# Two of the three inner dense layers of a graph-attention output stage by seven block products, and the last bias added to rows in DRAM

## The chip, the cores and the metric

The kernel runs on one NeuronCore of a Trainium2 chip. A core has a matrix engine (TensorE, PE in the profile; its weight loads are listed apart as PEld), a vector engine (DVE), a scalar engine that applies functions (ACT), a general engine that here mostly issues transfers (POOL, GpSimd), and an engine that issues transfers (SP). Each has its own instruction queue and works through it in order; they wait for one another by semaphores. Transfers go through 16 DMA engines. Data lies in DRAM, in the on-chip memory SBUF (128 partitions) and in PSUM, eight banks of 512 float32 per partition into which TensorE writes.

The metric is the device time of one execution in microseconds (us). Three runs of the kernel before gave 2115.71, 2116.22 and 2118.41 us; the median is 2116.22.

## The reference

Two residual layers on a graph of N = 3327 nodes with 1024 features. The first is a quantised graph convolution. The second, which the change touches, is a graph attention with 8 heads of 64 features, followed by four dense layers:

```python
def _L1_gnn_ref(x, adj, W, a1, a2, W1, b1, W2, b2, W3, b3, W4, b4):
    Wh = jnp.einsum('nf,hfd->hnd', x, W)
    ...
    att = jax.nn.softmax(e, axis=-1)
    h = jnp.einsum('hnm,hmd->hnd', att, Wh)
    h = jax.nn.elu(h)
    enc = jnp.transpose(h, (1, 0, 2)).reshape(x.shape[0], -1)   # 3327 x 512
    out = jax.nn.relu(enc @ W1.T + b1)                          # 512 -> 256
    out = jax.nn.relu(out @ W2.T + b2)                          # 256 -> 256
    out = jax.nn.relu(out @ W3.T + b3)                          # 256 -> 512
    out = out @ W4.T + b4                                       # 512 -> 1024
    return out
...
x = x + _L0_gnn_ref(h, adj, ...)
h = jnp.maximum(_layernorm(x, axis=-1), 0.0)
x = x + _L1_gnn_ref(h, adj, ...)
```

The result is x after the first layer (called x1 in the kernel, the other branch of the last addition) plus the output of the fourth dense layer with its bias b4.

## The kernel before

The 3327 rows lie in T = 26 tiles of 128. Three stages follow one another.

*First stage* (about 0 to 920 us): normalisation, quantised weights, and for each row tile the product with the adjacency matrix (L840) and the eight heads' products (L708). It writes x1 to DRAM as `x1_d`, tile by tile, on POOL's queue, and the heads' features and scores as `feat_d` and `src_d`.

*Attention* (about 895 to 1853 us). `attends` lists 8 heads times 4 sub-ranges of row tiles (7, 6, 7 and 6 tiles), 32 passes. Each pass goes through the 13 pairs of column tiles in 7 `GROUPS`. For a step (pass, group) the function `select` makes masks: ACT writes `over` (L969, two buffers of a pair each), DVE turns it into two selection tiles `sel` (L978 and L979, six buffers, one for a pair). `sums` multiplies the selections with the head's features on PE (L998) into one PSUM bank per row tile. `select` runs two steps ahead of `sums` (`AHEAD = 2`). When a pass ends, `closing` reduces the banks on DVE (L1017, L1022), applies the softmax's denominator and the ELU on ACT, and POOL's queue stores the encoded rows to `enc_d` (L1046). SP's queue loads the scores of the pass after the next (`load_src`, L933) and, once a head, the features of the next head (L918). The function `pin` chains the instructions of each engine in the order in which they are written out here; instructions outside `pin` are placed by the framework's scheduler. During the last pass SP loads what the output stage needs: encoded rows, x1 rows, weights, biases and, into `bb4`, the bias b4 broadcast to all partitions; two layers of group 0 are already computed between the sums (L1164), and `weight_sums` (L1196) makes differences of blocks of W4 on DVE.

*Output stage* (from 1853 us). The row tiles form 7 groups: 0 to 5 of four tiles (512 columns in the transposed layout), 6 of two (256 columns). Activations are transposed, features on partitions, nodes as columns. For each group `dense` computes the three inner layers h1, h2, h3: for each 128 output features one PSUM bank, one matmul call per 128 input features (L1238), and ACT adds the bias and applies the ReLU (L1248). h1 takes 8 calls, h2 4, h3 8; the profile shows two PE instructions for each call in float32.

The fourth layer is done by seven block products already, for a pair of row tiles at a time. `combined` (L1271 to L1274) makes four sums of the blocks of h3 on DVE, s1 to s4, once a group. `rows_out` first adds `bb4` to the two x1 tiles (L1289), then does the products in the order 1, 4, 2, 6, 7, 5, 3 (L1306, four PE instructions each), keeps products 1 and 6 in SBUF by way of ACT (L1308), and adds everything up on DVE (L1310 to L1322); `leave` (L1297) makes the finished half rows, which go out in transfers. The layers of the next group are put into the gaps of the present one: h1 after the third product of the first pair (called the gap at 2), h2 after its last, h3 after the third product of the second pair. In group 0 the next h1 comes first of all. ACT prepares the inputs of the group after the next (`joined`, L1259), and SP loads x1 rows of the next group (`load_x1`, L1139).

Of the kernel before, what the change touches and what calls it, by code (L numbers as in the profile page):

```python
# [22 lines left out]
P = 128  # L23
# [4 lines left out]
F = 1024  # L28
# [39 lines left out]
def two_layer_kernel(  # L68
# [105 lines left out]
    with tc.tile_pool(name="at", bufs=2, reuse_waits="tile") as atp:  # L174
# [47 lines left out]
        with tc.tile_pool(name="s1", bufs=2, reuse_waits="tile") as s1, tc.tile_pool(  # L222
# [9 lines left out]
            def pin(ins):  # L232
                tc.keep_in_program_order(ins)
# [663 lines left out]
    with tc.tile_pool(name="over", bufs=2, reuse_waits="tile") as overp, tc.tile_pool(  # L897
# [24 lines left out]
        def load_mask(si, js=slice(0, T), queue=nc.sync):  # L922
            for b, t in enumerate(SUBS[si]):
                ins = queue.dma_start(masks[si][:, b, js], mask_d[t][:, js])
            return ins

        srows = {}

        def load_src(i):
# [155 lines left out]
        for n, (i, g) in enumerate(steps):  # L1085
# [5 lines left out]
                load_src(i + 2)  # L1091
            if (i, g) == (1, 0):
                last_src()
            if (i, g) == (len(attends) - 1, 0):

                early.close()
                mlp = ctx.enter_context(ExitStack())

# [9 lines left out]
                rest = large(mlp, "rest", [P, 7 * NP // 4])  # L1108
                enc_x1.append(nodes("nodes1"))
                joined_1 = large(mlp, "joined_1", [P, EMB // P, 512])  # L1110
                bb4 = rest[:, :F]
                bb1, bb2, bb3 = (rest[:, F + 4 * q : F + 4 * q + 4] for q in range(3))
                h1_0, h2_0, enct0 = (
                    rest[:, F + 16 + 512 * at : F + 16 + 512 * (at + n)].rearrange("p (m c) -> p m c", c=512)
# [32 lines left out]
                        nc.sync.dma_start(bb[:, :m], ap.rearrange("(m p) -> p m", p=P))  # L1147
                w2, w3 = weight(w2t, D1 // P, D2), weight(w3t, D2 // P, D3)
                w4 = weight(w4t, D3 // P, F)
                nc.sync.dma_start(bb4, b4.partition_broadcast(P))  # L1150
                load_encoded(1, range(4, 8))

                def join(xt, enc, by_vector=()):
# [31 lines left out]
                    for n in range(3)  # L1185
                )
                t1 = w4c[0][1]

                def weight_sums():
                    for d, one, other in (  # L1190
                        (t3, w4c[1][1], w4c[0][1]),
                        (t1, w4c[0][1], w4c[0][0]),
                        (t2, w4c[1][1], t1),
                        (t4, w4c[1][0], t2),
                    ):
                        pin(nc.vector.tensor_tensor(d, one, other, ALU.subtract))  # L1196
# [16 lines left out]
                next(closed, None)  # L1213
            if (i, g) == (len(attends) - 1, 5):
                weight_sums()
                join(joined_1, enc_x1[1][0])

        for _ in closed:
# [3 lines left out]
    with tc.tile_pool(name="s4", bufs=2, reuse_waits="tile") as s4, tc.tile_pool(  # L1222
        name="s4_ps", bufs=4, space=PSUM, reuse_waits="tile"
    ) as ps_p, tc.tile_pool(name="s4_o", bufs=4, space=PSUM, reuse_waits="tile") as o_ps:

        groups = [range(t0, min(t0 + 4, T)) for t0 in range(0, T, 4)]

        def dense(xt, wt, bt, cols, tag, by_input=False):


            k_n, m_n = wt.shape[1], wt.shape[2] // P
            yt = s4.tile([P, m_n, 512], F32, tag=tag, name=tag)
            order = [(k, m) for m in range(m_n) for k in range(k_n)]
            pss = {}
            for k, m in sorted(order) if by_input else order:
                if k == 0:
                    pss[m] = ps_p.tile([P, 512], F32, tag="ps", name=f"{tag}_ps")
                ins = nc.tensor.matmul(  # L1238
                    pss[m][:, :cols],
                    wt[:, k, m * P : (m + 1) * P],  # L1240
                    xt[:, k, :cols],
                    start=(k == 0),
                    stop=(k == k_n - 1),
                )
                if by_input:
                    tc.keep_in_program_order(ins)
                if k == k_n - 1:
                    nc.scalar.activation(  # L1248
                        yt[:, m, :cols], pss[m][:, :cols], AF.Relu, bias=bt[:, m : m + 1]
                    )  # L1250
            return yt

        def joined(g):

            load_encoded(g % 2, groups[g])
            xt = s4.tile([P, EMB // P, 512], F32, name="enct")
            n = len(groups[g]) * P
            for k in range(EMB // P):
                nc.scalar.copy(halves_of_words(xt[:, k, :n]), by_feature(enc_x1[g % 2][0], n)[:, :, k])  # L1259
            return xt  # L1260

        sums = enct0.rearrange("p k c -> p (k c)").rearrange(
            "p (s k t i) -> p s k t i", s=4, k=2, t=2
        )

        def combined(h3, n):

            at = h3[:, :, : 2 * n * P].rearrange("p k (t e i) -> p k t e i", e=2, i=P)
            (a11, a21), (a12, a22) = [[at[:, 2 * k : 2 * k + 2, :, e] for e in range(2)] for k in range(2)]
            s1, s2, s3, s4_ = (sums[:, q, :, :n] for q in range(4))  # L1270
            pin(nc.vector.tensor_tensor(s1, a21, a22, ALU.add))  # L1271
            pin(nc.vector.tensor_tensor(s2, s1, a11, ALU.subtract))
            pin(nc.vector.tensor_tensor(s3, a11, a21, ALU.subtract))
            pin(nc.vector.tensor_tensor(s4_, a12, s2, ALU.subtract))  # L1274
            return {
                "1": (a11, w4c[0][0]),
                "2": (a12, w4c[1][0]),
                "3": (s4_, w4c[1][1]),
                "4": (a22, t4),
                "5": (s1, t1),  # L1280
                "6": (s2, t2),
                "7": (s3, t3),
            }

        def rows_out(tiles, x1, of, q, gaps):

            x0 = x1[:, q : q + 2]
            for e in range(2):
                pin(nc.vector.tensor_tensor(x0[:, e], x0[:, e], bb4, ALU.add))  # L1289
            (x11, x12), (x21, x22) = [  # L1290
                [x0[:, e, c * 512 : (c + 1) * 512] for c in range(FC)] for e in range(2)
            ]
            yo = [s4.tile([P, F], F32, name="yo", bufs=3) for _ in tiles]

            def leave(e, c, one, other):
                t, cs = tiles[e], slice(c * 512, (c + 1) * 512)
                nc.vector.tensor_tensor(yo[e][:, cs], one, other, ALU.add)  # L1297
                for queue, r in zip((nc.sync, nc.scalar), row_pieces(t)):
                    queue.dma_start(out[t * P + r.start : t * P + r.stop, cs], yo[e][r, cs])

            kept = {b: s4.tile([P, 512], F32, name="p" + b, bufs=1) for b in "16"}
            for n, b in enumerate("1426753"):
                st, mv = of[b]
                ps = o_ps.tile([P, 512], F32, tag="o", name="o")
                for k in range(2):
                    nc.tensor.matmul(ps, st[:, k, q // 2], mv[:, k], start=(k == 0), stop=(k == 1))  # L1306
                if b in kept:
                    nc.scalar.copy(kept[b], ps)  # L1308
                if b == "4":
                    nc.vector.tensor_tensor(x21, x21, ps, ALU.add)  # L1310
                elif b == "2":
                    nc.vector.tensor_tensor(x11, x11, ps, ALU.add)
                    leave(0, 0, kept["1"], x11)
                elif b == "6":
                    nc.vector.tensor_tensor(kept["6"], kept["6"], kept["1"], ALU.add)
                    nc.vector.tensor_tensor(x12, x12, kept["6"], ALU.add)
                elif b == "7":
                    nc.vector.tensor_tensor(kept["6"], kept["6"], ps, ALU.add)
                    nc.vector.tensor_tensor(x22, x22, kept["6"], ALU.add)
                    leave(1, 0, kept["6"], x21)  # L1320
                elif b == "5":
                    nc.vector.tensor_tensor(x12, x12, ps, ALU.add)  # L1322
                    leave(1, 1, ps, x22)
                elif b == "3":
                    leave(0, 1, ps, x12)
                if n in gaps:
                    gaps[n]()

        h3 = dense(h2_0, w3, bb3, len(groups[0]) * P, "h3")
        encs = {1: joined_1}  # L1330
        for g, tiles in enumerate(groups):
            following = []
            if g + 1 < len(groups):
                load_x1((g + 1) % 2, groups[g + 1])
                following = [(w1, bb1, "h1"), (w2, bb2, "h2"), (w3, bb3, "h3")]
                h = encs.pop(g + 1)

            def next_layer():
                nonlocal h
                wt, bt, tag = following.pop(0)  # L1340
                h = dense(h, wt, bt, len(groups[g + 1]) * P, tag)

            if g == 0:
                next_layer()
            of = combined(h3, len(tiles) // 2)
            at = [(0, 6), (1, 2)] if g == 0 else [(0, 2), (0, 6), (1, 2)]
            for pair in range(len(tiles) // 2):
                gaps = {n: next_layer for p, n in at if following and p == pair}
                rows_out(tiles[2 * pair : 2 * pair + 2], enc_x1[g % 2][1], of, 2 * pair, gaps)
                if pair == 0 and g + 2 < len(groups):  # L1350
                    encs[g + 2] = joined(g + 2)
            h3 = h
# [43 lines left out]
```

## Time and profile before

| what | value |
|---|---|
| time, median of 3 runs | 2116.22 us (2115.71 to 2118.41) |
| profiled execution: its own time | 2116.58 us |
| profiled execution: span | 2114.8 us |
| PE busy | 2080.0 us, 98% of the span |
| DVE busy | 1470.0 us, 70% |
| ACT busy | 1335.7 us, 63% |
| POOL busy | 169.2 us, 8% |
| DMA, mean | 110 GB/s |
| granted TensorE clock | 1.0 |

The span is what the profiler saw between the first and the last instruction; the execution's own time is 1.8 us longer. The table's busy times are averages over stages with different limits, so the stages are read one by one. In a chain of waits the work that ended last is followed back from the end of the kernel: each line has a start, a length, an engine, a tile, a line of the kernel and the number of instructions. In a group's line the busy time is followed by the mean in ns of one instruction, and then by the idle time of the engine just before these instructions with what ended it. A length is how long one instruction took from its start to its end; PE and DVE overlap the end of one with the start of the next, so the step from start to start is shorter.

### The profile page before, as it was taken

The numbers are of one execution on the slowest core, as the hardware profiler recorded it, in microseconds if no ns is written. First come the engines' busy times: TensorE is split into PE (matmuls) and PEld (weight loads), VectorE is DVE, ScalarE is ACT, GpSimd is POOL, SyncE is SP. The second block draws the span as 40 slices with busy tenths as digits, with TensorE's granted clock in tenths as the row PEclk, the third lists the DMA queues.
The fourth block names the chain that finished last, engine by engine and source line by source line (L and its number), as shares of the span: only waits on it lengthen the run. The fifth ranks groups of instructions, "written<-read, shape, count | busy, mean of one in ns | idle before, by whom it ended". The sixth has DMA issues, their size and how long they took to land.

```text
span 2114.8 us, 37954 instructions
## 1 busy us (share of the span) xinstructions
PE 2080.0 (98%) x15397; PEld 1740.9 (82%) x15397; DVE 1470.0 (70%) x2892; ACT 1335.7 (63%) x1816; POOL 169.2 (8%) x251
## 2 busy tenths in 40 slices
PE   5999999999999999999999999999999999999999
PEld 2468888888888888789999999999999999844444
DVE  8845677767666677687777777777777777655446
ACT  6733555454444555488888888888889888642321
POOL 2200000000010000200000000000000000000000
PEclk9999999999999999999999999999999999999999
DMA  6644665555456565690202021120212004443322
GB/s 216 178 144 137 166 171 151 140 137 156 140 148 161 166 171 153 181 296 26 75 26 73 19 71 26 26 75 18 71 26 75 26 21 132 113 118 117 114 85 75
DMA packets 195439, 233.62 MB, mean 110 GB/s; under 512 B 105188, under 2 KB 140116, under 8 KB 195264
## 3 DMA queue, kind: packets, MB, share of 16 engines
q1 hardware_dynamic: 179916, 176.92, 29.5%
q0 software_dynamic: 15280, 54.22, 9.1%
q8 instruction: 120, 1.97, 0.4%
q14 instruction: 55, 0.45, 0.1%
q10 hardware_dynamic: 68, 0.06, 0.0%
HBM read 141.74 MB, written 65.82 MB: 98 GB/s over the span
## 4 chain that ended last, share of the span: by engine, by line
PE 91%; DVE 3%; DMA 3%; ACT 2%; issue 1%; POOL 0%; SPq 0%; DVEq 0%; POOLq 0%; ACTq 0%
PE acc L998 41%; PE mm L840 28%; PE o L1306 7%; PE products L708 7%; PE h_ps L1238 5%; PE mm L348 3%; ACT over L969 1%; DMA feat_d<-fw 1%; PE h_ps L1164 1%; DMA xqt<-xq 1%; DMA yht<-yh 1%; DMA src_d<-srct 0%; DMA w<-in_w 0%; DVE stats L261 0%; ACT xb L320 0%
## 5 line engine op out<-in xcount | busy, mean ns | idle before, releaser
L998 PEld LDWEIGHTS <-sel 128*128 128x128 fp8e4 x10816 | 932.0, 97 | 8.7 <-issue 5.4
L969 ACT ACTIVATE over<-srow,large_dst 128x896 uint8<-128x896 f32 (+1 forms) x766 | 684.7, 975 | 30.1 <-DVE sel L978 30.1
L998 PE MATMUL acc<-f_even,sel 128*128 128x195 bf16 x5408 | 469.1, 247 | 2.6 <-DVE su L1017 1.5
L998 PE MATMUL acc<-f_odd,sel 128*128 128x195 bf16 x5408 | 467.4, 247 | 0.0
L840 PE MATMUL mm<-s_int,lo 128*128 128x512 f32 x1352 | 429.5, 395 | 0.0
L840 PE MATMUL mm<-s_int,hi 128*128 128x512 f32 x1352 | 426.1, 396 | 0.0
L978 DVE TENSOR_TENSOR sel<-over,mask 128x448 uint32<-128x448 uint32 (+1 forms) x416 | 243.9, 586 | 207.7 <-ACT over L969 115.9
L840 PEld LDWEIGHTS mm<-s_int,lo 128*128 128x128 f32 x1352 | 253.9, 188 | 52.5
L840 PEld LDWEIGHTS mm<-s_int,hi 128*128 128x128 f32 x1352 | 253.9, 188 | 51.8
L979 DVE TENSOR_TENSOR sel<-sel,mask 128x448 uint32<-128x448 uint32 (+1 forms) x416 | 246.0, 591 | 14.2
L191 ACT CAST hi<-at 128x512 fp32r<-128x512 f32 (+1 forms) x182 | 105.7, 587 | 152.0 <-PE mm L840 107.7
L195 DVE TENSOR_TENSOR lo<-at,hi 128x512 fp32r<-128x512 f32 (+1 forms) x182 | 117.7, 647 | 36.5 <-ACT hi L191 36.2
L1046 POOL DMA_DIRECT2D enc_d<-eh x64 | 57.7, 906 | 860.4 <-ACT eh L1044 859.9
L1031 ACT ACTIVATE ht<-su,rs 128x64 f32<-128x64 f32 x208 | 53.1, 335 | 108.6 <-DVE rs L1027 108.6
L1017 DVE TENSOR_REDUCE su<-acc 128x130 f32<-128x390 f32 x208 | 115.7, 556 | 7.9 <-PE acc L998 7.9
L1248 ACT ACTIVATE h<-h_ps,rest 128x512 f32<-128x512 f32 (+1 forms) x52 | 33.7, 654 | 118.7 <-PE h_ps L1238 118.7
L348 PE MATMUL mm<-w_int,xqt 128*128 128x512 bf16 x416 | 94.1, 382 | 7.0 <-DVE w_int L479 4.5
L625 ACT COPY yh<-y 128x1024 uint16<-128x1024 uint16 x50 | 51.9, 1038 | 57.9 <-DVE y L150 57.9
L348 PEld LDWEIGHTS <-xqt 128*128 128x128 bf16 x416 | 40.4, 99 | 55.6 <-issue 9.0
L635 ACT COPY ht<-yht 128x1024 uint16<-128x1024 uint16 x50 | 67.4, 1358 | 25.6 <-DMA yht<-yh 25.5
L196 DVE TENSOR_SCALAR mk<-at 128x512 uint8<-128x512 f32 (+1 forms) x182 | 72.5, 398 | 0.0
L1022 DVE SCALAR_TENSOR_TENSOR su<-su,ratio 128x65 f32<-128x65 f32 x208 | 59.7, 287 | 7.4
(251 smaller groups left out, 1935.0 us busy)
## 6 DMA issues: line engine op xcount, KB each, us to landing
at<-in_adj_t SPq DMA_DIRECT2D x130, 256.0 KB, 3.1
feat_d<-fw POOLq DMA_DIRECT2D x24, 780.0 KB, 7.9
x_d<-xt POOLq DMA_DIRECT2D x26, 512.0 KB, 3.7
nodes<-x_d SPq DMA_DIRECT2D x26, 512.0 KB, 4.8
xt<-in_x SPq DMA_DIRECT2D x25, 512.0 KB, 4.2
out<-yo SPq DMA_DIRECT2D x50, 256.0 KB, 2.0
xs<-in_x SPq DMA_DIRECT2D x24, 512.0 KB, 4.5
mask_d<-mk POOLq DMA_DIRECT2D x26, 416.0 KB, 3.9
```

The lines of the kernel that those rows point to most:

```text
L191: ins = high = nc.scalar.copy(hi, at)
L195: low = nc.vector.tensor_tensor(lo, at, hi.bitcast(F32), ALU.subtract)
L348: nc.tensor.matmul(mms[t][:, r], xqts[t][:, k, :], w_int[:, k, r], start=(k == 0), stop=(k == KF - 1))
L708: nc.tensor.matmul(ps, st[:, k], mv[:, k], start=(k == 0), stop=(k == KF // 2 - 1))
L840: nc.tensor.matmul(mm[:, c * 512 : (c + 1) * 512], which[:, q, :], s_int[j][:, c * 512 : (c + 1) * 512], start=(j == 0 and which is hi), s ...
L969: nc.scalar.activation(over[:, q], srows[i], AF.Relu, bias=large_dst[:, j, h : h + 1], scale=BIG)
L978: pin(nc.vector.tensor_tensor(up, over, of_pair, ALU.bitwise_and))
L979: ends["vector"] = pin(nc.vector.tensor_tensor(dn, up, of_pair, ALU.bitwise_xor))
L998: ins = nc.tensor.matmul(accs[i, b][:, r], chosen[i, pair][:, s, b, q], f[:, j, r], start=(j == 0 and s == 0), stop=(j == T - 1 and s == 1),)
L1017: nc.vector.tensor_reduce(su[:, b], accs.pop((i, b)).rearrange("p (q s c) -> p q c s", q=2, s=3), AX.X, ALU.add)
L1238: ins = nc.tensor.matmul(pss[m][:, :cols], wt[:, k, m * P : (m + 1) * P], xt[:, k, :cols], start=(k == 0), stop=(k == k_n - 1),)
L1306: nc.tensor.matmul(ps, st[:, k, q // 2], mv[:, k], start=(k == 0), stop=(k == 1))
```

## The change

Four things change.

1. In groups 1 to 6 the layers h1 and h3 no longer go through `dense` but through `dense_by_blocks`. Weight and activation are each cut into 2 x 2 blocks; seven products of blocks replace eight, in the order 1, 2, 6, 7, 5, 4, 3. Each product is two matmul calls over half the columns (256 in groups 1 to 5, 128 in group 6), in one bank of the same four. `moving` makes four differences of the activation's blocks on DVE for each layer (t3, b12 in its place, t2, t4); products 1, 2 and 3 use the blocks as they are (1 and 2 with unchanged weight blocks), 5 uses the new b12, 6 t2, 7 t3 and 4 t4. ACT copies product 1 to SBUF, seven additions on DVE (`plus`) put the products together, and ACT adds bias and ReLU from SBUF in place. h2, and all layers of group 0, stay as they were.
2. `stationary` makes four sums of the weight's blocks for W1 and W3, eight additions on DVE, right behind `weight_sums` in the last pass of the attention. They lie where `bb4` was and in a part of the mask memory that is free by then.
3. The bias b4 is no longer added in `rows_out`. During the attention, at the step of group 3 of passes 2 to 27, `add_bias` loads one tile of x1 from DRAM on SP's queue, adds the bias on DVE, and stores it back on POOL's queue. The broadcast of b4 is loaded once, at the second pass, into a buffer that is given up at the last pass.
4. h1 and h2 have one buffer in place of two.

On DVE the additions of `add_bias` and `stationary` are pinned, and so are the differences; the `plus` additions are placed by the scheduler, which also mixes them with the additions of the output.

```diff
--- before.py
+++ after.py
@@ -924,6 +924,18 @@
+        biasing = ExitStack()
+        biased = biasing.enter_context(tc.tile_pool(name="biased", bufs=2, reuse_waits="tile"))
+        bias = biased.tile([P, F], F32, name="bias", bufs=1)
+
+        def add_bias(t):
+
+            xb = biased.tile([P, F], F32, name="xb1")
+            rows = slice(t * P, (t + 1) * P)
+            nc.sync.dma_start(xb, x1_d[rows])
+            pin(nc.vector.tensor_tensor(xb, xb, bias, ALU.add))
+            nc.gpsimd.dma_start(x1_d[rows], xb)
+
         srows = {}
@@ -1091,8 +1103,12 @@
                 load_src(i + 2)
             if (i, g) == (1, 0):
                 last_src()
+                nc.sync.dma_start(bias, b4.partition_broadcast(P))
+            if g == 3 and 0 <= i - 2 < T:
+                add_bias(i - 2)
             if (i, g) == (len(attends) - 1, 0):
 
+                biasing.close()
                 early.close()
@@ -1108,7 +1124,7 @@
-                bb4 = rest[:, :F]
+                sums_1 = rest[:, :F].rearrange("p (n k m) -> p n k m", n=4, k=2)
@@ -1147,7 +1163,6 @@
-                nc.sync.dma_start(bb4, b4.partition_broadcast(P))
@@ -1185,6 +1200,33 @@
+                sums_3 = masks[3].rearrange("p b j i -> p (b j i)").bitcast(F32)[:, 3 * F : 4 * F].rearrange(
+                    "p (n k m) -> p n k m", n=4, k=1
+                )
+
+                def blocks(wt):
+                    k, m = wt.shape[1] // 2, wt.shape[2] // 2
+                    return [[wt[:, i * k : (i + 1) * k, c * m : (c + 1) * m] for i in range(2)] for c in range(2)]
+
+                def stationary(wt, sums):
+
+                    (a11, a12), (a21, a22) = blocks(wt)
+                    s1, s2, s3_, s4_ = (sums[:, n] for n in range(4))
+                    pin(nc.vector.tensor_tensor(s1, a21, a22, ALU.add))
+                    pin(nc.vector.tensor_tensor(s2, s1, a11, ALU.subtract))
+                    pin(nc.vector.tensor_tensor(s3_, a11, a21, ALU.subtract))
+                    pin(nc.vector.tensor_tensor(s4_, a12, s2, ALU.subtract))
+                    return {"1": a11, "2": a12, "3": s4_, "4": a22, "5": s1, "6": s2, "7": s3_}
+
+                def moving(xt, cols, store):
+
+                    (b11, b21), (b12, b22) = blocks(xt[:, :, :cols])
+                    t2, t3, t4 = (store[:, n, :, : cols // 2] for n in range(3))
+                    pin(nc.vector.tensor_tensor(t3, b22, b12, ALU.subtract))
+                    pin(nc.vector.tensor_tensor(b12, b12, b11, ALU.subtract))
+                    pin(nc.vector.tensor_tensor(t2, b22, b12, ALU.subtract))
+                    pin(nc.vector.tensor_tensor(t4, b21, t2, ALU.subtract))
+                    return {"1": b11, "2": b21, "3": b22, "4": t4, "5": b12, "6": t2, "7": t3}
@@ -1213,6 +1255,7 @@
                 weight_sums()
+                of_1, of_3 = stationary(w1, sums_1), stationary(w3, sums_3)
                 join(joined_1, enc_x1[1][0])
@@ -1229,7 +1272,7 @@
-            yt = s4.tile([P, m_n, 512], F32, tag=tag, name=tag)
+            yt = s4.tile([P, m_n, 512], F32, tag=tag, name=tag, bufs=1 + (tag == "h3"))
@@ -1250,6 +1293,52 @@
+        def dense_by_blocks(xt, of, bt, cols, tag):
+
+            k_n, m_n, n = xt.shape[1] // 2, of["1"].shape[2] // P, cols // 2
+            store = s4.tile([P, 3, k_n, 256], F32, name=f"{tag}_t", bufs=1)
+            moved = moving(xt, cols, store)
+            yt = s4.tile([P, 2 * m_n, 512], F32, tag=tag, name=tag, bufs=1 + (tag == "h3"))
+            (c11, c12), (c21, c22) = [
+                [yt[:, i * m_n : (i + 1) * m_n, c * n : (c + 1) * n] for c in range(2)] for i in range(2)
+            ]
+            p1 = s4.tile([P, m_n, 256], F32, name=f"{tag}_p", bufs=1)[:, :, :n]
+
+            def product(b):
+                ps = ps_p.tile([P, 512], F32, tag="ps", name=f"{tag}_ps")
+                ps = ps[:, : m_n * n].rearrange("p (m n) -> p m n", m=m_n)
+                for m in range(m_n):
+                    for k in range(k_n):
+                        nc.tensor.matmul(
+                            ps[:, m],
+                            of[b][:, k, m * P : (m + 1) * P],
+                            moved[b][:, k],
+                            start=(k == 0),
+                            stop=(k == k_n - 1),
+                        )
+                return ps
+
+            def plus(out, one, other):
+                nc.vector.tensor_tensor(out, one, other, ALU.add)
+
+            def finish(rows):
+                for m in rows:
+                    y = yt[:, m, :cols]
+                    nc.scalar.activation(y, y, AF.Relu, bias=bt[:, m : m + 1])
+
+            nc.scalar.copy(p1, product("1"))
+            plus(c11, p1, product("2"))
+            plus(c12, p1, product("6"))
+            plus(c21, c12, product("7"))
+            p5 = product("5")
+            plus(c22, c21, p5)
+            plus(c12, c12, p5)
+            plus(c21, c21, product("4"))
+            finish(range(m_n, 2 * m_n))
+            plus(c12, c12, product("3"))
+            finish(range(m_n))
+            return yt
@@ -1285,8 +1374,6 @@
             x0 = x1[:, q : q + 2]
-            for e in range(2):
-                pin(nc.vector.tensor_tensor(x0[:, e], x0[:, e], bb4, ALU.add))
@@ -1332,13 +1419,14 @@
-                following = [(w1, bb1, "h1"), (w2, bb2, "h2"), (w3, bb3, "h3")]
+                following = [(of_1, bb1, "h1"), (w2, bb2, "h2"), (of_3, bb3, "h3")]
...
-                h = dense(h, wt, bt, len(groups[g + 1]) * P, tag)
+                layer = dense if tag == "h2" else dense_by_blocks
+                h = layer(h, wt, bt, len(groups[g + 1]) * P, tag)
```

## The prediction

> **What bounds the kernel now.** I read the page's chain first, then the chain in order of time over the last stage, the windows of the attention and the last stage, who waits for whom in the attention, and the groups by shape.
>
> ```profile
> PE 91%; DVE 3%; DMA 3%; ACT 2%; issue 1%; POOL 0%; SPq 0%; DVEq 0%; POOLq 0%; ACTq 0%
> ```
>
> TensorE ends the chain nearly everywhere. One group of four row tiles in the last stage, in order of time (start, length, line, instructions), and the two layers of group 6:
>
> ```profile
> 1935.19 12.02 PE o L1306 x28
> 1947.21 6.87 PE h_ps L1238 x16
> 1954.08 6.87 PE o L1306 x16
> 1960.94 3.43 PE h_ps L1238 x8
> 1964.38 5.15 PE o L1306 x12
> 1969.53 6.87 PE h_ps L1238 x16
> ...
> 2070.81 3.45 PE h_ps L1238 x16
> ...
> 2088.01 3.45 PE h_ps L1238 x16
> ```
>
> A float32 matrix product is two PE instructions here (8 calls are x16); I call each a pass. A pass over 512 columns takes 6.87/16 = 0.429 us, over 256 columns 3.45/16 = 0.216. Each group takes 41.2 us (1935.19 to 1976.39) without a gap, 20.6 in the three inner layers and the first and third of them 6.87 each.
>
> ```profile
> 1250.00:1350.00 100.00, 100.00 (x1164) 100.00 (x1162) 74.11 (x147) 84.15 (x111) 5.24 (x6) 1.00 0.19 51
> ...
> 1852.00:2100.00 248.00, 248.00 (x606) 114.00 (x605) 133.25 (x193) 72.18 (x105) 1.65 (x2) 1.00 0.32 99
> ```
>
> Columns: length, busy PE, PEld, DVE, ACT, POOL, granted clock, DMA share, GB/s. PE is full in both stages at full clock; DVE has 26% free in the attention, 46% in the last stage.
>
> ```profile
> DVE sel L978 <- ACT over L969: 104.4, 158, 1.3
> ...
> DVE sel L978 <- PE acc L998: 87.0, 58, 2.6
> ```
>
> In the 853 us of steady attention DVE waits 87.0 us, in 58 waits, because all six selection buffers are full: it is then as far ahead of PE as it can get.
>
> **The change part by part.** *The layers.* In groups 1 to 5 the first and third layer each become 7 products of 4 passes over 256 columns: 28 x 0.2156 = 6.04 us for 6.87, 0.83 saved, ten times: **8.3 us**. Group 6 has 256 columns, so its passes cover 128. No row has a float32 matmul of that width. If time follows columns it is half of 0.216, 28 x 0.108 = 3.02 for 3.45, so 0.86 gained in the two layers. If the weight load's own length sets the pace it is 28 x 0.190 = 5.32, so 3.7 lost:
>
> ```profile
> L1238 PEld LDWEIGHTS h_ps<-enct,weights 128*128 128x128 f32 x80 | 15.2, 190 | 16.1 <-issue 15.8
> ...
> 902.57 0.42 PEld L650 LDWEIGHTS tp<-ident,y 128*128 128x128 f32 x4 [0.86 <-DVE lnv L152]
> 902.57 0.66 PE L650 MATMUL tp<-ident,y 128*128 128x128 f32 x4 [0.63 <-DVE lnv L152]
> ```
>
> The nearest row is the transposes: four loads of 0.140 us fit into 0.42 (one every 0.093), so a load's length is not its pace; four matmuls over 128 columns take 0.66, each 0.27 long, one every 0.130. I take 0.130: 28 x 0.13 = 3.64, so 0.19 lost per layer, **0.4 us**. The Trainium skill (TensorE: Matmul & The Clock Gate, "LDWEIGHTS") puts a load at columns/1.2 ns, 107 ns for 128, well under the 190 of the row; by it the passes would run near the half price and the total would be 1.3 us lower than mine; no row here shows a load's share of the array by itself, and the spacing of 0.093 leans to the page.
>
> *What DVE must deliver in a group.* Today DVE has 26 operations over 512 (0.685 each; L1271 to L1274 and eleven per pair) and 4 bias adds of 1.216 (L1289): 22.7 us of 41.2. The adds leave; in come four differences for the first layer (512 wide, 2.8), four for the third (256 wide, 0.425 as L1271 in group 6: 1.7), seven sums of 256 (3.0) and seven of 512 (4.8): 30.1 of a new period 41.2 - 1.7 = 39.5. Room is there; the question is the moment. Count from a group's first o product, in the order in which the changed program has them on DVE. Products 1, 4, 2 end at 5.15, the first layer's products 1 and 2 (which need no sum) at 6.88, output product 6 at 8.60; then PE needs difference t2. On DVE the add for product 2 starts 0.2 after 5.15 (L1312 starts at 1969.57, the product ended at 1969.36), then come a difference, a leaving add, and t2, at 0.605 us from start to start (L1322 at 1941.02, L1297 at 1941.62): t2 is ready at 5.36 + 3 x 0.605 + 0.69 = 7.9, **0.7 us early**. Before that DVE must be through: the seven sums of the third layer end at 33.6, the ReLUs on ACT at 35.6, then the copy of p6 (0.58) eight operations to 1.5 us after the next group's start, and there four sums for the output and two more, to 5.3. It just fits. The third layer is easier: h2's last ReLU ends about 22.3, t2 at 23.7, needed at 28.4. The output sums s1 to s4 are needed from 6.9 on and the second is ready at 3.0. The seven products share four PSUM banks; the fifth needs the first one's copy by ACT, done 1.8 us before. So **0** on PE; should the chain slip, about 0.5 us in each of five groups.
>
> *Sums of weights*, 8 adds of 0.425 = 3.4 us on DVE behind L1196, in a gap:
>
> ```profile
> 1849.37 0.56 DVE L1017 TENSOR_REDUCE su<-acc 128x130 f32<-128x390 f32 x1 [7.92 <-PE acc L998]
> ```
>
> **0**; without the gap the closing sums of the last attention slip 3.4 and PE, which waits for one of them (0.28), with them. In group 1 the differences follow DVE's L1037, end 1857.7, so t2 is there about 1859.7, before products 1 and 2 run (from 1859.5 to 1861.2).
>
> *Bias in the attention*: 26 adds of 1.216 us on DVE, 31.6 in all, one per attended pass of 26.7 us, behind the selections of group 5. Queued behind each are the next selections, for which PE would wait. The cover: 87.0/30 = 2.9 us a pass waiting for a free selection buffer and 3.5 waiting for ACT's masks, together 6.4 > 1.22. ACT may run two pairs ahead and has 1.7 us of work a pair, so it is not held. I take **0**; bounds 0 and 31.6. Transfers: 27 loads of 512 KB on SP (a broadcast of the bias, 5.4 us in the row of today, which leaves the last stage; 26 tiles, 4.8 us as nodes<-x_d) and 26 stores on POOL. Loads wait for the store of two tiles earlier; behind them on SP stand the score rows, wanted a full pass later, and the features of the next head, wanted four passes later. On POOL stand the enc_d stores, and POOL waits 789 of these 853 us for ACT. DMA share is 0.19. The last tile is written about four passes before the output stage reads it. **0**. Taking the adds out of the last stage frees DVE, not PE, which has no gap there: 0.
>
> **Sum.** 8.3 - 0.4 = 7.9 us. The profiled execution has a span of 2114.8 and took 2116.58, 1.8 outside the span; the median of the runs is 2116.22. 2116.58 - 7.9 = 2108.7; against the median 2108.3. I predict **2108.5 us**.
>
> **Rivals.** (a) *The handover becomes the bound.* t2 comes late because dependent operations go at 0.72 to 0.79 (L1315 to L1316, L1316 to L1318) and the previous group's sums run over. Six operations at 0.79 are 1.1 later than at 0.605: 0.5 late in five groups, 2.5 us, 2111. For it: the 0.7 us of margin is the least in the stage. Against: each group starts anew from PE's clock.
> (b) *Slower than before: the adds in the attention reach PE.* Place: DVE between two selections. Were each add paid in full, 31.6 - 7.9 = 23.7 us more, 2140; it turns slower from 0.30 us per add (7.9/26). For it: after the closing sums DVE's lead shrinks (at the change of head at 1258.8 the timeline has pair 5 ready at 1264.9, and PE, two groups of 4.6 us on, gets there about 1267.9) and ACT is 85% busy. Against: the full-buffer waits above come in every pass, after each add and before the next closing.
> (c) *Loads set group 6's pace*: 0.190 a pass, 3.7 in place of 0.4: 2111.9. For: the load row. Against: the transposes.
> (d) *Loads are not hidden behind matmuls at all in the short passes*, so that a pass costs 0.216 + 0.190: 28 x 0.406 = 11.4 for 6.87, ten times 4.5, and in group 6 28 x 0.298 = 8.3 for 3.45, twice 4.9: 55 us more, 2171. Against it speak 16 passes with their loads in 3.45 us. The same page (Part 3, "The mechanism") says loads overlap running matmuls only where the row groups differ, which would be this case; the trace disagrees, 0.216 a pass with a load of 0.190 for each.
>
> **Chances.** Forecast 0.68 (its own range 2107.1 to 2110), (a) 0.11, (b) 0.12, (c) 0.07, (d) 0.02. The 80% range drops (b) and (d) beyond their beginnings: 2106.5 to 2114. Low end: group 6 at half price, 2107.1 against the median, and a little for run noise. High end: (a) and (c) together, or a sixth of (b). A measurement tells 0.2%, 4.2 us, from no change. The forecast is faster; so are (a) and (c), except where they coincide or add to a small (b). Faster 0.81, within 0.2% 0.06, slower 0.13.
>
> **What would show it.** Right: first and third layer x28 in about 6.04 us without a gap, group period 39.5; the adds' line in the attention with PE still at 100.00 in a 100 us window; waits of L978 for PE shorter by about 1.2 a pass. Wrong: PE idle before the block products released by DVE (a); PE idle before acc released by sel (b); group 6 layers over 5 us (c); 256-column passes over 0.216 (d).

## The result, and the profile after

The changed kernel takes 2109.34 us (median of 5 runs, 2106.67 to 2110.0), the kernel before beside it 2117.03 us (5 runs, 2115.71 to 2118.41). The ratio is 0.9961, with a 95% interval of 0.9946 to 0.9976 that excludes 1: faster, by 7.7 us or 0.4%.

The profiled execution took 2108.81 us with a span of 2106.8 us, against 2116.58 and 2114.8: 8.0 us less span. The chain in order of time says where they come from. The output stage begins at 1852.94 (before: 1852.77) and TensorE's chain ends at 2096.50 (2082.75 + 13.75; before: 2105.21). The stage lasts 243.56 us instead of 252.44: 8.88 less. At the very end 0.7 us are given back: from the end of DVE's last sum to the end of the span it is 4.3 us (2102.46 to 2106.8) instead of 3.6 (2111.18 to 2114.8). 8.88 - 0.7 - 0.17 (the later begin) = 8.0.

The chain of one steady group of the changed kernel, and the first and third layer of group 6 (start, length, line, instructions; L1312 are the block products, L1281 the second layer, L1393 the output products):

```profile
1926.03 6.04 PE h_ps L1312 x28
1932.08 12.02 PE o L1393 x28
1944.09 1.73 PE h_ps L1312 x8
1945.82 1.72 PE o L1393 x4
1947.53 4.32 PE h_ps L1312 x20
1951.85 5.15 PE o L1393 x12
1957.00 3.43 PE h_ps L1281 x8
1960.43 5.15 PE o L1393 x12
...
2062.75 0.89 PE h_ps L1312 x8
...
2065.36 2.23 PE h_ps L1312 x20
...
2079.62 3.12 PE h_ps L1312 x28
```

Each piece starts where the one before ends: there is no gap, the third layer is x28 in 6.04 us and the first x8 and x20 in 6.05, and the next group begins at 1965.58, a period of 39.55 us. In group 6 a layer of 28 passes takes 3.12 us, where 16 passes took 3.45. No wait of PE's products is listed in the output stage.

The same stretch of the attention as before, and nearly the same of the output stage (length, busy PE, PEld, DVE, ACT, POOL, clock, DMA share, GB/s):

```profile
1250.00:1350.00 100.00, 100.00 (x1164) 100.00 (x1163) 77.16 (x151) 84.31 (x111) 6.93 (x9) 1.00 0.31 91
1852.00:2090.00 238.00, 238.00 (x749) 136.56 (x748) 165.13 (x299) 75.97 (x117) 1.65 (x2) 1.00 0.34 104
```

PE is as full as before. In the attention DVE has 3.1 us more in 100 and the DMA share rises from 0.19 to 0.31; in the output stage DVE goes from 54% to 69%. The waits in the attention, from 967 to 1820 us (engine, line, for whom: us in all, times, longest):

```profile
POOL x_d L937 <- DVE xb L936: 106.8, 26, 4.5
...
DVE sel L990 <- PE acc L1010: 86.9, 58, 2.6
DVE sel L990 <- ACT over L981: 76.2, 106, 1.3
```

The 26 adds (L936, 1.218 us each, 31.7 in all) cost PE nothing. They did not come out of DVE's waits for a full set of selection buffers (87.0 us before, 86.9 now) but out of its waits for ACT's masks, 104.4 before and 76.2 now: 28.2 of the 31.7.

### The profile page after: what moved, and what is told of

Same layout as the page of the kernel before. It is cut to its first block, busy times and chain, and to the rows that moved or that the text cites. A ratio compares the mean times of both kernels' runs of the same rounds, so it can differ in the third digit from the quotient of the medians.

```text
span 2106.8 us, 38597 instructions
## 1 busy us (share of the span) xinstructions
PE 2071.1 (98%) x15541; PEld 1763.5 (84%) x15541; DVE 1531.9 (73%) x3032; ACT 1339.5 (64%) x1828; POOL 183.9 (9%) x277
## 4 chain that ended last, share of the span: by engine, by line
PE 92%; DVE 3%; DMA 2%; ACT 2%; issue 1%; POOL 0%; SPq 0%; DVEq 0%; POOLq 0%; ACTq 0%
PE acc L1010 41%; PE mm L840 28%; PE o L1393 7%; PE products L708 7%; PE h_ps L1312 3%; PE mm L348 3%; PE h_ps L1281 1%; ACT over L981 1%; DMA feat_d<-fw 1%; PE h_ps L1179 1%; DMA w<-in_w 0%; DMA yht<-yh 0%; DVE stats L261 0%; DMA xqt<-xq 0%; DVE w_stats L391 0%
## 5 line engine op out<-in xcount | busy, mean ns | idle before, releaser
L981 ACT ACTIVATE over<-srow,large_dst 128x896 uint8<-128x896 f32 (+1 forms) x766 | 684.7, 975 | 32.2 <-DVE sel L990 30.1
L1029 DVE TENSOR_REDUCE su<-acc 128x130 f32<-128x390 f32 x208 | 115.7, 556 | 5.0 <-PE acc L1010 5.0
L793 ACT ACTIVATE ratio<-srcs 128x8 f32<-128x8 f32 x26 | 5.4, 209 | 88.2 <-DVE srcs L788 88.2
```

The lines of the kernel that those rows point to most:

```text
L981: nc.scalar.activation(over[:, q], srows[i], AF.Relu, bias=large_dst[:, j, h : h + 1], scale=BIG)
L1029: nc.vector.tensor_reduce(su[:, b], accs.pop((i, b)).rearrange("p (q s c) -> p q c s", q=2, s=3), AX.X, ALU.add)
```

## Experiments

The kernels of the first three sections below ran beside the kernel before at 2115.65 us (2113.7 to 2116.54, 15 runs); for the others the time beside them is given in the text. "Stage" is the output stage in the chain, "end" the time from DVE's last sum to the end of the span.

| kernel | median us (runs) | ratio to before | stage us | end us |
|---|---|---|---|---|
| before | see the text | 1 | 252.44 | 3.6 |
| changed, first runs | 2109.34 (5) | 0.9961 [0.9946, 0.9976] | 243.56 | 4.3 |
| changed, again | 2108.62 (5) | 0.9968 [0.9956, 0.9981] | 243.56 | 4.4 |
| blocks only | 2107.35 (5) | 0.9959 [0.9946, 0.9973] | 244.39 | 3.7 |
| bias only | 2116.70 (11) | 1.0005 [0.9996, 1.0014] | 252.4 | 4.4 |
| second layer too | 2105.22 (5) | 0.9952 [0.9939, 0.9964] | 241.34 | 4.3 |
| two adds | 2111.19 (7) | 0.9970 [0.9959, 0.9982] | 243.56 | 4.4 |
| three adds | 2130.35 (4) | 1.0063 [1.0049, 1.0077] | 243.56 | 4.3 |
| five adds | 2197.14 (1) | none | 243.55 | 4.4 |
| all blocks, old bias | 2108.24 (5) | 0.9958 [0.9944, 0.9971] | 243.25 | 3.7 |
| add in three parts | 2107.62 (1) | none | 241.34 | 4.0 |

### The changed kernel again

> The changed kernel once more, beside the three below. Theory (PE passes saved in the inner layers, nothing lost elsewhere): 7.5 to 9 us less than the kernel before, first and third layers 6.04 us each in groups 1 to 5 and 3.12 in group 6. A rival that the first gain was partly chance of the runs gives a difference under 6 us.

7.0 us less than the kernel before, 2108.62 against 2115.65: half a microsecond short of the range expected, and over the 6 us that would have spoken for chance. Its stage is the same to the hundredth. Its attention happened to start 1.4 us later (969.32 against 967.92), as such starts do from run to run; medians of one or two us apart are therefore read together with the stage.

### The two halves of the change

Blocks only: the layers as changed, the bias added in the output stage as before.

```diff
-        def add_bias(t):
...
-            if g == 3 and 0 <= i - 2 < T:
-                add_bias(i - 2)
...
+                bb4 = rest[:, :F]
...
+            for e in range(2):
+                pin(nc.vector.tensor_tensor(x0[:, e], x0[:, e], bb4, ALU.add))
```

> The block products stay, the bias is added in the output stage as before. Theory (the bias adds cost DVE time that the output stage can still spare: 35 of 39.5 us a group): the output stage on PE is as long as in the changed kernel to within 1 us, the time 7 to 9 us below the kernel before, and the differences of the first layer come with a margin under 0.7 us. Rival (the bias adds, 2.4 us ahead of t2, eat the 0.67 us of margin that the trace shows): PE waits for DVE up to 1.7 us in each of five groups, up to 8.5 us in all, so the time is 2108 + 8.5 = 2117, no better than before.

2107.35 us: all of the gain is there without the moved bias. The chain of its steady group shows what the returned adds do:

```profile
1944.12 1.73 PE h_ps L1302 x8
1945.85 4.29 PE o L1385 x10
1950.14 4.50 PE h_ps L1302 x20
```

Ten passes of the output product stand between block products 2 and 6 where the changed kernel has four (the scheduler puts others there while DVE is busy), and the 20 passes take 4.50 us instead of 4.32: 0.18 a group. The rival of the expectation has the mechanism: the bias adds do use up the margin. The difference t2 (L1217) now ends at 1949.94, after the 1947.37 at which the changed kernel starts the products that need it, and these products start at 1950.09, as soon as it is there. The six further output passes, 2.57 us, stand where PE would have waited, so 0.18 is left of the 1.7 us a group that the rival feared. The stage is 0.83 longer than in the changed kernel, and the end is 0.6 to 0.7 shorter. The two cancel.

Bias only: the adds in the attention, all layers as before.

```diff
+            if g == 3 and 0 <= i - 2 < T:
+                add_bias(i - 2)
...
-            for e in range(2):
-                pin(nc.vector.tensor_tensor(x0[:, e], x0[:, e], bb4, ALU.add))
```

> The bias in the attention, all inner layers as before. Theory: neither the 26 adds in the attention nor their absence in the output stage reaches PE, so the time is that of the kernel before within 1.5 us and PE's attention lasts as long to within 0.3 us. Rival (the adds cost PE some of their 31.6 us): each tenth that is paid shows as 3 us more. Rival (PE waited for the bias adds in the output stage): 1 to 3 us less.

2116.70 us, ratio 1.0005 with 1 inside the interval: the move alone is worth nothing, as predicted. The stage is as long as in the kernel before, and all that it costs in the trace is the end, 4.4 us against 3.6.

### The second layer by blocks too

```diff
-                of_1, of_3 = stationary(w1, sums_1), stationary(w3, sums_3)
+                of_1, of_2, of_3 = stationary(w1, sums_1), stationary(w2, sums_2), stationary(w3, sums_3)
...
-                layer = dense if tag == "h2" else dense_by_blocks
-                h = layer(h, wt, bt, len(groups[g + 1]) * P, tag)
+                h = dense_by_blocks(h, wt, bt, len(groups[g + 1]) * P, tag)
```

> The second inner layer of groups 1 to 6 by seven block products as well: 14 passes over 256 columns, 3.02 us for 3.43, in five groups, and 14 over 128 at 0.1115, 1.56 for 1.73, in group 6: 2.2 us less on PE, if DVE's 4.7 us more a group (34.8 of 39.1) stay behind it: 2107 us against 2109. Rival (the handover from one layer to the next is now the bound, the second layer's sums and differences being between the first and the third): PE idle before block products, 0.5 us or more a handover in 12 handovers, 6 us more: 2113.

2105.22 us (2105.02 to 2106.43), below every run of the changed kernel beside it (2107.61 to 2110.22): it beats both kernels. One group of its chain:

```profile
1941.68 1.73 PE h_ps L1313 x8
...
1945.12 4.32 PE h_ps L1313 x20
...
1954.59 0.86 PE h_ps L1313 x4
1955.45 1.72 PE o L1394 x4
1957.17 2.16 PE h_ps L1313 x10
```

The second layer is now 14 passes over 256 columns, 0.86 + 2.16 = 3.02 us for 3.43, again without a gap. Period 39.14, stage 241.34, which is 2.22 less than the changed kernel's: what the passes give. The medians differ by 3.4; the other 1.2 is within what the start of the attention moves from run to run (966.34 and 969.32 in the two traces).

### Where the cover in the attention ends

How many adds does a pass of the attention hide? The added instructions stand behind the add in each of the 26 passes. With three and five the bias is added and taken away in turn, with two the second takes the larger of the row and itself, so the rows that are stored hold the bias once. The kernels with three and five adds, and those of the two sections after this one, ran beside the kernel before at 2117.06 us (9 runs), the one with two adds beside 2117.73 (10 runs).

```diff
-            pin(nc.vector.tensor_tensor(xb, xb, bias, ALU.add))
+            for n in range(3):
+                pin(nc.vector.tensor_tensor(xb, xb, bias, ALU.subtract if n % 2 else ALU.add))
```

> The changed kernel with the bias added, taken away and added again in each of the 26 passes of the attention that add it: three adds of 1.22 us on VectorE, 3.65 us a pass, 2.43 us a pass and 63 us in all more than in the changed kernel. Theory A (the prediction's cover, 6.4 us of VectorE's idle time a pass, is all to be had): no change, 2108 to 2110 us. Theory B (only the waits of VectorE between the add and the next closing count, some 3.4 us in the stretch read before: 0.5, 0.5, 0.7, 0.6, 0.7, 0.4): 0 to 0.2 us a pass late, 0 to 5 us in all, 2109 to 2114 us. The waits of the masks for ScalarE's (76.2 us in all after the change) should fall by most of the 63 us.

> The changed kernel with five adds of 1.22 us on VectorE in each of the 26 passes, 6.1 us a pass, 4.87 us a pass and 127 us in all more than in the changed kernel. Theory A (cover of 6.4 us a pass): no change, 2108 to 2110 us, TensorE's chain of the attention 855 us as now. Theory B (cover of some 3.4 us a pass): 2 to 2.65 us a pass come through to TensorE, which waits for the closing to give its banks back: 50 to 70 us, 2160 to 2180 us, and a wait of the sums for the closing line appears in the list.

Both theories were wrong in size: 2130.35 us with three, 2197.14 with five (one run). The wait of the sums for the closing line, which theory B expected, is there. The output stage of both starts late by what the span has grown, 1874.54 and 1941.25 against 1852.94: 21.6 and 88.3 us, 0.83 and 3.40 a pass. The waits in the attention with three adds:

```profile
DVE sel L991 <- ACT over L982: 75.3, 133, 1.3
ACT over L982 <- DVE sel L991: 51.2, 27, 2.0
DVE sel L991 <- PE acc L1011: 39.4, 41, 2.6
PEld L1011 <- issue: 14.2, 14, 1.1
PE acc L1011 <- DVE su L1030: 12.0, 13, 0.9
```

and the moment of one such pass (start, length, what; in brackets the idle time before it and who ended it):

```profile
1254.24 3.74 DVE L937 TENSOR_TENSOR xb<-xb,bias 128x1024 f32<-128x1024 f32 x3
...
1258.48 10.37 ACT L982 ACTIVATE over<-srow,large_dst 128x896 uint8<-128x896 f32 x11 [2.04 <-DVE sel L991]
...
1267.28 0.56 DVE L1030 TENSOR_REDUCE su<-acc 128x130 f32<-128x390 f32 x1
...
1267.89 0.33 PE L1011 MATMUL acc<-f_odd,sel 128*128 128x195 bf16 x2 [0.91 <-DVE su L1030]
```

While DVE adds, it takes no mask away, both `over` buffers stay full, and ACT stands for 2.04 us. Afterwards DVE waits for ACT in turn at every pair, so the lost time is not caught up; the last pair and the closing sums come late, and PE waits 0.91 us for a bank that they have to empty. In the changed kernel ACT's wait of this kind is 28.1 us in 29 times and no longer than 1.4, just as in the kernel before; with five adds it is 115.7 us. The waits of the masks for ACT, which were expected to fall by most of 63 us, stay at 75.3.

The chain of waits over the same stretch, 1240 to 1330 us, says it most plainly. In the changed kernel it is

```profile
by line: PE acc L1010 100.0%
```

and with three adds

```profile
by line: ACT over L982 47.4%; DVE su L1030 10.8%; DVE xb L937 8.3%; issue 7.2%; DVE su L1035 6.4%; DVE sel L991 6.0%; ACT ht L1044 5.0%; ACT eh L1057 2.6%; DVE sel L992 2.1%; ACT ex L1046 1.9%; ACT ex L1047 1.9%; DVE rs L1040 0.7%
```

With three adds PE is no longer in the chain at all: ACT and DVE, each in turn waiting for the other, have become the bound. From the add of one pass to the add two passes later it is 59.8 us there (1254.24 to 1314.08) and 58.2 in the changed kernel (1158.40 to 1216.62), which is 0.81 a pass. PE's listed waits, 13 of them, come in every second pass; 0.83 is the mean.

The two further adds from three to five cost 3.40 - 0.83 = 2.57 us a pass for 2.43 us of work: past the edge nearly one for one. (With five adds pieces of PE are in the chain again, some of them at a lower clock, as the last section shows; so that kernel is not a clean measure of the slope.) Drawn back from there, the edge lies at 3.65 - 0.83 = 2.8 us a pass. That asks for a test between one and three.

> The changed kernel with a second VectorE instruction of the same size behind each add of the attention (the larger of each row and itself, so the rows stay as they are): 2.44 us a pass. Three such instructions (3.65 us) cost 21.6 us of span, 0.83 us a pass, five (6.1 us) cost 88.4 us, 3.40 us a pass: the two more add 2.57 us a pass for 2.43 us of work, nearly one for one. Theory A (a sharp edge: VectorE has 3.65 - 0.83 = 2.8 us a pass to give): two cost nothing, the same time as the changed kernel (2108 to 2110.5 us), no wait of the sums for the closing line. Theory B (the reserve runs out gradually, from one add on): 10 us more, 0.35 to 0.4 us a pass (2118 to 2120 us), with such waits in the list. Beside it the end of the kernel: 26 more instructions on VectorE. If the crossing into a new piece of its instructions makes the 0.7 us at the end, no such packet is seen in the last 4 us, and the time from VectorE's last sum to the end of the span is 3.6 to 4.0 us instead of 4.3.

2111.19 us, above the 2108 to 2110.5 expected, but a ratio of 0.9970, within the two intervals of the changed kernel (the kernel before was slower beside it, too). In its trace the output stage starts at 1853.31, no wait of PE for the closing line is listed in the attention, and from 1000 to 1700 us the chain is PE's products alone. The trace is of the fastest of the seven runs, so a loss of a microsecond or two in the others is not excluded; a loss of 10, theory B's, is. The edge lies between 2.44 and 3.65 us a pass, where the chain passes from PE to ACT and DVE. The waits for ACT do not fall with the work: 96.4 us in this kernel, more than with one add (76.2), while those for a free buffer go from 86.9 to 36.4.

### All layers by blocks, the bias in the output stage

```diff
-                following = [(of_1, bb1, "h1"), (w2, bb2, "h2"), (of_3, bb3, "h3")]
+                following = [(of_1, bb1, "h1"), (of_2, bb2, "h2"), (of_3, bb3, "h3")]
...
-                layer = dense if tag == "h2" else dense_by_blocks
-                h = layer(h, wt, bt, len(groups[g + 1]) * P, tag)
+                h = dense_by_blocks(h, wt, bt, len(groups[g + 1]) * P, tag)
```

(against the kernel with the blocks only)

> All three inner layers of groups 1 to 6 by seven block products, and the bias added in the output stage as before the change. VectorE has 31.9 us of work in a steady group with the first and third layer by blocks and the old bias; the second layer adds 31.4 - 27.8 = 3.6 us: 35.5 us beside 39.1 us of TensorE. Theory A (VectorE keeps up, moving the bias is worth nothing even here): as the kernel with all layers by blocks and the bias in the attention, 2104.5 to 2106.5 us, no wait of TensorE for a combination over 0.2 us a group. Theory B (this is where the moved bias pays: the combinations of the second layer queue behind the bias adds): TensorE waits 0.3 us a group and more for them, 2107 us and above, and the 2.2 us of the second layer are lost again.

2108.24 us beside 2117.06, 8.8 less; the kernel with the bias in the attention had 10.4 less than the 2115.65 beside it. The stage tells it more sharply: 243.25 us, 1.91 longer than with the moved bias. DVE is busy 35.3 us of a group of 39.4, and PE's weight loads now wait for ReLUs:

```profile
PEld h_ps L1300 <- ACT h L1315: 3.8, 9, 0.9
```

Some of these ReLUs stand behind DVE's sums (the load at 1926.21 waits 0.52 us for one that had waited 1.12 for a sum), but before the longest wait, 0.88 us at 1958.40, ACT was busy with its copy of a later group's inputs (L1336) for 1.34 us from 1955.81 on, while DVE had finished its sums at 1956.23. So theory B is right in time and in part in mechanism, and theory A's 2104.5 to 2106.5 was missed; of the second layer's 2.2 us half is lost, not all (244.39 to 243.25 is 1.14). Of the kernels tried the moved bias pays only here, by 1.9 us of the stage less 0.7 at the end. This rests on the traces: the intervals of the two ratios (0.9939 to 0.9964 and 0.9944 to 0.9971) overlap.

### The end of the kernel

```diff
-            pin(nc.vector.tensor_tensor(xb, xb, bias, ALU.add))
+            for c in (slice(0, 384), slice(384, 768), slice(768, F)):
+                pin(nc.vector.tensor_tensor(xb[:, c], xb[:, c], bias[:, c], ALU.add))
```

(on the kernel with all layers by blocks and the bias in the attention)

> All three layers by blocks and the bias in the attention, with each of the 26 adds cut in three parts of 384, 384 and 256 columns: 52 more instructions on VectorE, far from the end, with the same columns. It asks where 0.7 us at the very end come from: from the end of VectorE's last sum to the end of the span it is 3.6 us in the kernel before and in the one with the block products alone, 4.3 us in the three kernels with the bias in the attention; those three show a packet of instructions fetched in the last 4 us, the other two none. Theory A (VectorE's list of instructions crosses a piece of its fetch there): 52 more instructions move the crossing away, the end is 3.6 us again and the packet is gone from the last 4 us. Theory B (it is something else of the moved bias, such as its transfers or their closing): 4.3 us stay. Total 2104 to 2106 us in either.

The time, 2107.62 us in one run, is above the 2104 to 2106 expected; the stage is that of the kernel it was made from, 241.34, and the attention starts 3.0 us later than in that kernel's trace (969.30 against 966.34). The end is 4.0 us here, between the two, and the packet is gone. This row of the DMA view, over the last 4 us, is there in all seven other traces with the bias in the attention (the last figure is 0.6 to 0.9%), and in none of the three without:

```profile
q14 instruction: 1, 0.01, 0.6%
```

That the packet and the longer end go together is shown (4.3 to 4.4 us with it in seven traces, 3.6 to 4.0 without in four). Whether the packet causes the longer end, and what sets it off, is not: with 26, 52 and 104 more instructions on DVE (two, three and five adds) the packet is still there, so a count of DVE's instructions alone does not explain it. It stays open, at 0.7 us.

## Why the prediction was right, and which of its steps were not

The forecast, 2108.5 us, stands 0.8 below the measured 2109.34. Its main term, the passes saved on a full PE, is right in mechanism and size; three smaller steps were not. By its steps:

- *The layers of groups 1 to 5, 8.3 us*: right. 28 passes in 6.04, no gap, period 39.55 (worked out: 39.5).
- *Group 6, 0.4 us lost*: wrong in size and sign, the term of the sum that was mis-sized. A pass over 128 columns takes 3.12/28 = 0.1115 us, not 0.130; a layer gains 0.33, the two 0.66. The low bound (0.108, time by columns) was the good one; the transposes, taken as the nearest row, were not a fair price for a pass in a row of 28. With it the sum for the stage would have been 8.3 + 0.66 = 8.96 against 8.88 measured. By the Trainium skill (TensorE: Matmul & The Clock Gate, "LDWEIGHTS"), from whose columns/1.2 the prediction had the estimate of 107 ns for a load of 128 columns, the half price was allowed; the trace is in keeping with it, 0.1115 us a pass with a load in each.
- *The end*: no term for it. The 0.7 us given back there hid most of the 1.06 by which group 6 came out better. So the total is nearer than its terms: two errors of opposite sign, which is luck.
- *DVE in a group*: right in the moment that mattered; the work, 30.1 us added up from lengths, is 27.8 busy in the trace, since neighbouring operations overlap. Difference t2 of the first layer ends at 1946.70 and its products start at 1947.37, 0.67 us early (predicted 0.7):

```profile
1946.02 0.68 DVE L1227 TENSOR_TENSOR h_t<-enct 128x512 f32<-128x512 f32 x1
...
1947.37 1.89 PE L1312 MATMUL h_ps<-h_t,rest 128*128 128x256 f32 x8
```

- *Sums of weights and transfers at nothing*: nothing of either is seen. The output stage starts 0.17 us later than before; the DMA share rose by 0.12 in the attention with PE still at 100.00.
- *The adds in the attention at nothing*: the price was right, the cover was not. "Together 6.4" fails: three adds, 3.65 us a pass, already reach PE. The step that broke is "ACT may run two pairs ahead [...], so it is not held". It is held, already in the kernel before (28.1 us in 29 waits) and for 2.04 us in the pass shown, and then DVE's waits for ACT are no time to spare but the price of ACT's own wait for DVE. What was to be had is 2.4 to 2.8 us a pass, close to the 2.9 of the full-buffer waits; that this is more than chance is not shown, since 39.4 us of them are still there when PE already waits. The pass that an add has to hide in is 29.1 us long, not 26.7 (26 adds from 984.5 to 1712.6). That the adds would shorten these waits by 1.2 a pass was wrong, too: with one add it is the waits for ACT that shrink (28.2 us), with two the waits for a buffer shrink by 50.5 and those for ACT grow by 20.2, 30.3 less in all for 31.7 us more work.
- *Taking the adds out of the output stage at nothing*: right for the change as a whole (blocks only is as fast). It is worth 0.8 us of the stage with two layers by blocks and 1.9 with three.
- *Rivals*: (a) fell, PE waits for no difference in the changed kernel; its mechanism is seen where the old bias is kept, with two layers by blocks (0.18 us a group) and with three. (b) fell for one add; it begins between 2.4 and 3.65 us a pass. Its place was not quite right: with three adds PE waits for the closing sums (12.0 us), for selections only with five (11.5, beside 41.8 for the closing sums). (c) fell with 0.1115 us a pass over 128 columns, (d) with 6.04 for 28 passes over 256. The rule named with (d), from the same page of the Trainium skill (Part 3, "The mechanism"), that loads overlap running matmuls only where the row groups differ, disagrees with this trace also at the shortest pass: 28 passes, each with its own load, in 3.12 us. The text above that rule in the same section also has a background weight buffer, whose loads go ahead of running matmuls; that would allow it, and no run here shows whether it applies.

## What to carry to other kernels

Seven block products in place of eight pay on a full TensorE as long as the vector engine can deliver the differences a few operations ahead of the product that needs them: read that moment from the trace, not the engine's mean load. Idle time of an engine that waits for a partner, which waits for it in turn, must not be added up as cover; add the suspected work in steps (here one, two, three and five adds) and see where the bound engine starts to wait and drops out of the chain. Where one part of a change serves another (here the bias moved to make room on DVE), try each alone: the move bought nothing until all three inner layers were done by blocks and filled the vector engine.

## What the runs showed of the hardware that was not expected

- A float32 pass over 128 columns with its own 128x128 load takes 0.1115 us in a row of 20 or 28, though the load's record is 0.192 long: so the records of neighbouring loads overlap each other as well as the matmuls.
- With PE waiting up to 3.2 us in every second pass (five adds, one run) the granted clock fell: the mean of the run is 0.989, and 0.97 to 0.98 in windows of 100 us of the attention where it was 1.00 with one add. Behind the wait of 3.17 us that ends at 1228.28 it reads 0.54, 0.50, 0.50 and 0.75 in the four windows of 1 us from 1229 on, and 1.00 before and after. With waits of 0.91 (three adds) it stayed at 1.00.
- A packet of instructions fetched after DVE's last sum, in the last 4 us, goes with 0.3 to 0.8 us more at the end of the kernel. Its trigger was not found, and that it is the cause is not shown.
